# Layer norm of a macaron block: moments on ScalarE, reciprocal roots by GpSimd powers, and other places in the instruction order

## The chip, the cores and the metric

The kernel runs on one core of a Trainium2 chip. The core has five engines, each with its own instruction queue that is worked off in order: TensorE (PE in the profile, with its weight loads as PEld), VectorE (DVE), ScalarE (ACT), GpSimd (POOL) and SyncE (SP), which here issues the DMA transfers. An engine that waits for a semaphore holds everything behind it in its queue. The metric is the device time of one execution in microseconds, lower being better.

## The reference

The input is x, 2048 tokens of 512 float32 numbers. Three residual steps are computed:

```python
x = x + 0.5 * ffn(layernorm(x))
x = x + attention(layernorm(x))
x = x + 0.5 * ffn(layernorm(x))        # the same weights again

def layernorm(x): return (x - mean(x)) / sqrt(var(x) + 1e-5)

def ffn(x):       # Wg, Wu: 4096 x 512, Wd: 512 x 4096, each from 4-bit codes and a scale per 32 numbers
    gate, up = x @ Wg.T, x @ Wu.T
    return (gelu_tanh(gate) * up) @ Wd.T

def attention(x): # 16 heads of 32, causal softmax
    q, k, v = split(x @ Wqkv.T + bqkv)
    return softmax(q @ k.T / sqrt(32) + causal) @ v @ Wout.T + bout
```

Only the layer norms and the order of the work around them are touched by the change.

## The kernel before

**Tokens and phases.** The 2048 tokens are 16 tiles of 128 tokens (`xs`), and four blocks `tb` of 512 tokens (four tiles each). x stays in SBUF throughout. Three phases follow one another: `ffn(1, ...)`, `attention(...)` and `ffn(2, ...)`. Every phase starts from normalized and transposed tokens, `xT[tb]`.

**The norm of a block.** `norm_steps` returns a list of ten closures. `stats(0)` and `stats(2)` compute mean and variance of two tiles each on DVE (`bn_stats`, L88, and `bn_aggr`, L89); the second one then takes the square root of the four variances on ACT (L95), the reciprocal on DVE (L96) and, when the normalization is to run on ACT, minus mean times reciprocal on DVE (L98). `normalize(i)` writes the normalized tile `xn` (ACT at L105, or DVE at L107), into one of two buffers. `transpose(i)` transposes it by four matrix instructions into a PSUM bank (L115), which ACT copies into `xT` (L116). ACT holds one set of function tables at a time; the square root, GELU and exponential are in different sets, and each change of set shows as an `ACT_TABLE_LOAD`.

**An FFN phase.** The hidden size is cut into eight groups `g` with two halves each (`rows` and `second`), and the tokens into two pairs of blocks (`tp` 0: blocks 0 and 1, `tp` 1: blocks 2 and 3). `slot(g, rows, tp, ...)` computes gate and up of one half for one pair with Strassen's seven products instead of eight, so a slot has 14 products: seven for gate (`pg`, in the order 1, 2, 6, 7, 5, 4, 3) and seven for up (`pu`). A product is two calls, four matrix instructions of 128x512 in the profile, and takes one of seven PSUM banks (`ps_one`), which all phases share with the transposes. The right-hand factors are sums of token blocks, computed by `token_sums(tp)` on DVE (L256 to L259); products 1 and 2 need only the first block, product 6 needs the third sum. The products are combined by additions on DVE (L318 to L336), two copies on ACT (u2 after product 1, L315, with a single buffer; u4 after product 5, L327) and one addition on GpSimd (L330); GELU on ACT (L296) ends a gate cell and a multiplication with it on DVE (L300) ends an up cell.

In phase 1 the weights are first dequantized from their codes: ten steps on DVE per matrix half (L194 to L190), then four sums on GpSimd (L234 to L237). The weights are stored to DRAM and phase 2 reads them back, so that DVE and GpSimd have less to do there. Later halves are dequantized in the `background`: `slot` calls `pump(rate)` after every product, which takes so many steps from that list. `slot` also takes `groups`, lists of closures, and runs one group after each product. The down product is cut into 14 pieces (`down_pieces`, `po`, L375) that are either interleaved with a slot's products (`fill`) or, at the phase's end, run alone, with groups from `behind(normed)` between them.

**Where the norms stand.** At the start of phase 1 blocks 0 and 1 are normalized between the dequantization steps of the first half. The norms of blocks 2 and 3 are run by the groups `last_norms` of the second slot (`second`, pair 0), in the order that `paced` writes out: `[a0], [a1], [b0], [b1, an[0]], [an[1], at[0]], ...`, so moments, roots, normalizations and transposes all fall into that slot, and the token sums of pair 1 follow with its last product. Phase 2 does the same; its blocks 0 and 1 were normalized at the end of attention. The first two blocks of attention are normalized behind the last down pieces of phase 1 (`norms_behind`, also `paced`), and the first two blocks of phase 2 among the last steps of attention (L919 to L925), between the exponentials of the scores (L833) and the multiplications that form `attnT` (L779, on GpSimd, after reciprocals on DVE, L776). There the normalization is on DVE.

**Order.** The program is scheduled by hand: the order in which the Python code issues instructions is the order in each engine's queue. Waits are only added where data or buffers demand them.

## Time and profile before

| | us |
|---|---|
| median of three runs | 3295.69 |
| lowest and highest | 3292.89, 3295.72 |
| the profiled execution, its own time | 3295.73 |
| its span in the profile | 3294.0 |
| mean granted TensorE clock, share of full | 0.996 |

The page of the profile was taken on this one execution. Its first part gives the busy time of each engine; its second part cuts the span into 40 slices of 82 us. DVE is fullest in phase 1:

```profile
DVE  7877777877777556575655664554455455445545
ACT  4111111111111131464544455431111111111111
DMA  3111111111111100000000000101011101011101
```

Each digit is a busy share in tenths. Phase 1 takes slices 1 to 15, attention ends near the 26th, and phase 2 takes the rest. The most frequent instructions are these groups (line, engine, operation, output and inputs, count, then busy us, mean ns and the idle time ahead of them):

```profile
L375 PE MATMUL po<-wd,inter 128*128 128x256 f32 x2048 | 483.6, 380 | 0.0
L276 PE MATMUL pg<-xT_f,w 128*128 128x512 f32 x1024 | 480.9, 598 | 0.0
```

Matrix instructions are pipelined: four of one product are issued every 0.43 us, so a product takes 1.72 us though each one lasts some 0.6 us.

### The profile page before, as it was taken

How to read it: one execution, taken by the hardware profiler on the slowest of the kernel's cores; microseconds unless marked ns; L12 is line 12 of the kernel's file. 1: busy time of each engine (PE TensorE's matmuls, PEld its weight loads, DVE VectorE, ACT ScalarE, POOL GpSimd, SP SyncE). 2: the span in 40 equal slices, each digit the busy share in tenths (PEclk: the TensorE clock that was granted, in tenths of full speed). 3: DMA queues.
4: the chain of work that ended last, by engine and by line, in shares of the span. 5: the costliest groups of instructions: out<-in, count | busy, mean ns of one | idle time of the engine just before them, and what ended most of it. 6: DMA issues, size and time to landing. Idle time of an engine off the chain costs nothing.

```text
span 3294.0 us, 34151 instructions
## 1 busy us (share of the span) xinstructions
PE 3248.1 (99%) x12656; PEld 1724.3 (52%) x12656; DVE 2042.2 (62%) x3152; ACT 872.7 (26%) x1802; POOL 1127.8 (34%) x1319
## 2 busy tenths in 40 slices
PE   7999999999999999999999999999999999999999
PEld 3556565655656565333344333346555565656556
DVE  7877777877777556575655664554455455445545
ACT  4111111111111131464544455431111111111111
POOL 2546464554646331332212223113132222313222
PEclk9999999999999999999999999899999999999999
DMA  3111111111111100000000000101011101011101
GB/s 134 62 57 64 64 48 64 67 54 62 64 64 47 69 17 7 12 8 6 14 3 8 29 21 8 49 23 37 31 45 45 45 23 45 29 39 45 45 23 51
DMA packets 42055, 134.15 MB, mean 41 GB/s; under 512 B 5864, under 2 KB 26344, under 8 KB 35360
## 3 DMA queue, kind: packets, MB, share of 16 engines
q1 hardware_dynamic: 41888, 131.96, 11.0%
q8 instruction: 100, 1.64, 0.2%
q14 instruction: 67, 0.55, 0.1%
HBM read 81.91 MB, written 48.46 MB: 40 GB/s over the span
## 4 chain that ended last, share of the span: by engine, by line
PE 93%; DVE 3%; ACT 2%; issue 1%; POOL 1%; DMA 0%; SPq 0%; POOLq 0%; DVEq 0%; ACTq 0%
PE po L375 23%; PE pu L276 23%; PE pg L276 22%; PE av L740 8%; PE pm L675 6%; PE pqk L586 4%; PE ps L801 2%; PE pv L603 2%; PE pp L625 2%; PE ps L810 2%; ACT pt L833 1%; DVE st_f L88 0%; PE pt_f L115 0%; PE pt_a L115 0%; ACT both L749 0%
## 5 line engine op out<-in xcount | busy, mean ns | idle before, releaser
L375 PE MATMUL po<-wd,inter 128*128 128x256 f32 x2048 | 483.6, 380 | 0.0
L276 PE MATMUL pg<-xT_f,w 128*128 128x512 f32 x1024 | 480.9, 598 | 0.0
L276 PE MATMUL pu<-xT_f,w 128*128 128x512 f32 x1024 | 476.0, 592 | 0.0
L375 PEld LDWEIGHTS po<-wd,inter 128*128 128x128 f32 x2048 | 389.6, 190 | 155.4 <-issue 104.7
L690 DVE TENSOR_REDUCE parts<-pm 128x1 f32<-128x512 f32 (+3 forms) x640 | 370.4, 607 | 149.9 <-PE pm L675 134.6
L330 POOL TENSOR_TENSOR u<-u,u 128x512 f32<-128x512 f32 x128 | 163.7, 1279 | 865.5 <-ACT u L327 861.2
L389 POOL TENSOR_TENSOR x<-x,d 128x512 f32<-128x512 f32 x248 | 329.2, 1338 | 345.0 <-DVE d L383 171.7
L375 PE MATMUL po<-wd,s 128*128 128x256 f32 x1536 | 362.3, 379 | 0.0
L276 PE MATMUL pg<-xsum,w 128*128 128x512 f32 x768 | 357.4, 595 | 3.9 <-issue 2.0
L276 PE MATMUL pu<-xsum,w 128*128 128x512 f32 x768 | 355.7, 592 | 0.0
L375 PEld LDWEIGHTS po<-wd,s 128*128 128x128 f32 x1536 | 291.7, 190 | 116.2 <-issue 79.2
L675 PE MATMUL pm<-kT,qT 32*128 32x512 f32 (+3 forms) x1280 | 334.1, 574 | 0.1
L833 ACT ACTIVATE pt<-ps 128x512 f32<-128x512 f32 (+3 forms) x576 | 271.8, 533 | 130.3 <-PE ps L810 128.4
L740 PE MATMUL av<-pt,vaug 128*64 128x512 f32 (+3 forms) x1280 | 302.4, 557 | 3.1 <-ACT both L749 2.5
L276 PEld LDWEIGHTS pg<-xT_f,w 128*128 128x128 f32 x1024 | 195.8, 192 | 195.6 <-issue 181.8
L276 PEld LDWEIGHTS pu<-xT_f,w 128*128 128x128 f32 x1024 | 194.0, 190 | 189.9 <-issue 180.3
L810 PE MATMUL ps<-qT,kT 32*128 32x512 f32 (+3 forms) x1280 | 280.3, 539 | 0.0
L276 PEld LDWEIGHTS pg<-xsum,w 128*128 128x128 f32 x768 | 146.2, 191 | 151.5 <-issue 139.2
L276 PEld LDWEIGHTS pu<-xsum,w 128*128 128x128 f32 x768 | 145.5, 190 | 142.4 <-issue 135.4
L383 DVE SCALAR_TENSOR_TENSOR x<-po,x 128x512 f32<-128x512 f32 x192 | 131.4, 685 | 114.7 <-ACT d L397 85.6
L827 POOL TENSOR_SCALAR_AFFINE_SELECT pt<-pt 128x256 f32<-128x256 f32 x128 | 52.0, 406 | 401.2 <-ACT pt L826 400.4
L383 DVE SCALAR_TENSOR_TENSOR d<-po,d 128x512 f32<-128x512 f32 x192 | 131.6, 686 | 83.9 <-PE po L375 83.2
(128 smaller groups left out, 3601.6 us busy)
## 6 DMA issues: line engine op xcount, KB each, us to landing
kept<-wd SPq DMA_DIRECT2D x8, 1792.0 KB
wd<-kept SPq DMA_DIRECT2D x8, 1792.0 KB
x<-in_x SPq DMA_DIRECT2D x16, 256.0 KB
pk<-in_gate_codes SPq DMA_DIRECT2D x16, 256.0 KB
sc<-in_gate_scales SPq DMA_DIRECT2D x32, 128.0 KB
pk<-in_up_codes SPq DMA_DIRECT2D x16, 256.0 KB
sc<-in_up_scales SPq DMA_DIRECT2D x32, 128.0 KB
pk<-in_down_codes SPq DMA_DIRECT2D x16, 256.0 KB
```

The costliest lines, as they stand in the source:

```text
L276: nc.tensor.matmul(ps, lhsT=a[:, j, :], rhs=b[:, j, :], start=(j == 0), stop=(j == 1))
L330: nc.gpsimd.tensor_tensor(u4, u4, u2, ALU.add)
L375: nc.tensor.matmul(ps[:, j, :], lhsT=a[i][:, k, bass.ts(2 * q + j, P)], rhs=b[i][:, k, :], start=(k == 0), stop=(k == 1),)
L383: stt(dst, ps, 0.5, other, ALU.mult, ALU.add)
L389: adder.tensor_tensor(dst, dst, other, ALU.add)
L586: nc.tensor.matmul(ps, lhsT=w[:, j, k, :], rhs=xT[tb][:, k, :], start=(k == 0), stop=(k == 3))
L603: nc.tensor.matmul(ps[:, i, :], lhsT=xT[t // 4][:, k, (t % 4) * P : (t % 4 + 1) * P], rhs=wv_sb[:, k, bass.ts(half, 256)], start=(k == 0), ...
L675: nc.tensor.matmul(ps[a][:, :n], lhsT=q[r, bass.ts(4 * g + i, P)], rhs=k[r, kb * 512 : kb * 512 + n], start=True, stop=not on_pe,)
L690: nc.vector.tensor_reduce(parts[:, a, i, kb : kb + 1], ps[a][:, :n], AX.X, ALU.max)
L740: nc.tensor.matmul(av[64 * a : 64 * a + 64, off:], lhsT=vaug[:, c, p % 4, HD * a : HD * a + 2 * HD], rhs=pt[:, a, off:], start=(c == 0), s ...
L810: nc.tensor.matmul(ps[a][:, off:], lhsT=k[r, bass.ts(c, P)], rhs=q[r, g * 512 + off : (g + 1) * 512], start=False, stop=True,)
L833: nc.scalar.activation(pt[:, a, plain:], ps[a][:, plain:], AF.Exp, scale=scale)
```

## The change

`norm_steps` and `paced` become a class `Norm` with lists `moments`, `scales`, `normal` and `transposed`, and a function `staggered`, which interleaves two blocks' normalizations and transposes. New options are `moments_on_act` (sums and squared deviations as ACT instructions with an accumulated output, instead of `bn_stats` on DVE), `power` (the reciprocal root as an addition and a power -0.5 on GpSimd, instead of root on ACT and reciprocal on DVE), and `on_act` as the tiles that ACT normalizes.

```diff
+    expo = const.tile([P, 4], F32, tag="expo", name="expo")
+    nc.gpsimd.memset(expo, -0.5)
...
+        def __init__(self, phase, tb, t_out, temp, on_act=(0, 1, 2, 3), moments_on_act=False, power=False):
...
+            if moments_on_act:
+                def sums():
+                    for i in range(4):
+                        nc.scalar.activation(temp(f"sum_{nm}_{i}"), tiles[i], AF.Identity, accum_out=total[:, i : i + 1])
+                    nc.scalar.activation(total, total, AF.Identity, scale=-1.0 / D)
+                def squares():
+                    for i in range(4):
+                        nc.scalar.activation(
+                            temp(f"sq_{nm}_{i}"), tiles[i], AF.Square, bias=total[:, i : i + 1],
+                            accum_out=square[:, i : i + 1],
+                        )
+                self.moments = [sums, squares]
...
+            def scales():
+                if power:
+                    if moments_on_act:
+                        nc.gpsimd.tensor_scalar(rstd, square, 1.0 / D, EPS, ALU.mult, ALU.add)
+                    else:
+                        nc.gpsimd.tensor_scalar(rstd, mv[:, :, 1], EPS, None, ALU.add)
+                    nc.gpsimd.tensor_tensor(rstd, rstd, expo, ALU.pow)
+                    if moments_on_act:
+                        nc.gpsimd.tensor_tensor(nbias, total, rstd, ALU.mult)
+                    elif on_act:
+                        nc.gpsimd.tensor_scalar(nbias, mv[:, :, 0], -1.0, None, ALU.mult)
+                        nc.gpsimd.tensor_tensor(nbias, nbias, rstd, ALU.mult)
+                else:
+                    nc.scalar.activation(rstd, mv[:, :, 1], AF.Sqrt, bias=eps)
+                    nc.vector.reciprocal(rstd, rstd)
...
+    def staggered(a, b):
+        n, t = a.normal + b.normal, a.transposed + b.transposed
+        return [[n[0]]] + [[n[i + 1], t[i]] for i in range(7)] + [[t[7]]]
```

The other half of the diff changes where things are issued. In phase 1 the x tiles of block 1 are loaded ahead of the codes; block 1's moments come right behind block 0's norm, its normalizations (two on ACT, two on DVE) between the gate steps, and the token sums ahead of the up steps. Moments and scales of blocks 2 and 3 go into the first slot (`early`), their normalizations and transposes into the second from its first product on (`late`), with the token sums as groups of that slot. The down dequantization is put into the background before the second slot, at one step a product.

```diff
             if phase == 1:
+                load_x(1)
                 rows.load(0)
-                load_x(1)
                 rows.load(1)
...
-                run(norms[0][:2])
+                n0 = Norm("f1", 0, xT[0], normed)
+                n1 = Norm("f1", 1, xT[1], normed, on_act=(0, 1), power=True)
                 gate, up = rows.steps(0), rows.steps(1)
-                run(gate[:4])
-                run(norms[0][2:])
-                run(gate[4:])
-                run(norms[1][:2])
-                run(up[:4])
-                run(norms[1][2:])
-                run(up[4:10])
-                run(token_sums(0))
-                run(up[10:])
+                run(n0.steps() + n1.moments + [n1.scales] + gate[:5] + n1.tiles() + gate[5:])
+                run(token_sums(0) + up)
...
-            last_norms = paced(norms[2], norms[3])
-            sums = token_sums(1)
-            last_norms = [[]] + last_norms
-            last_norms[-1].append(sums[0])
-            last_norms.append(sums[1:])
+            n2, n3 = [
+                Norm(f"f{phase}", tb, xT[tb], normed, moments_on_act=True, power=True) for tb in (2, 3)
+            ]
+            early = [[]]
+            for n in (n2, n3):
+                early += [[n.moments[0]], [], [n.moments[1]], [], [n.scales]]
+            late = staggered(n2, n3) + [[s] for s in token_sums(1)]
...
-                    first = [slot(g, rows, 0, *fill, 2)]
+                    first = [slot(g, rows, 0, *fill, 2, early)]
                     pump(1 << 30)
-                    last = [slot(g, second, 0, [], [], 0, last_norms)]
...
+                if g == 0:
+                    last = [slot(g, second, 0, [], [], 1, late)]
-                first.append(slot(g, rows, 1, [], [], 1 if g > 0 else 2))
+                first.append(slot(g, rows, 1, [], [], 1))
```

At the two other seams, the end of phase 1 and the end of attention:

```diff
     def norms_behind(temp):
...
-        return paced(*[norm_steps("a", tb, xT_a[tb], temp, True) for tb in range(2)])
+        a, b = [Norm("a", tb, xT_a[tb], temp) for tb in range(2)]
+        tiles = staggered(a, b)
+        tiles[1].append(b.moments[1])
+        tiles[2].append(b.scales)
+        def scaled():
+            a.moments[1]()
+            a.scales()
+        return [[], [a.moments[0]], [scaled], [b.moments[0]]] + tiles
...
-                        steps = norm_steps(
-                            "f2", tb, xT_f[tb], lambda nm: an.tile([P, D], F32, tag="xn", name=nm)
+                        norm = Norm(
+                            "f2", tb, xT_f[tb], lambda nm: an.tile([P, D], F32, tag="xn", name=nm), (), power=True
                         )
-                        for i, step in enumerate(steps):
+                        for i, step in enumerate(norm.steps()):
```

Blocks 2 and 3 of attention use `Norm` with the old operations in the old order.

## The prediction

> **What bounds the kernel now.** I read the page first (busy shares and slices), then who PE waited for, then the timeline at each place where PE stops.
>
> ```profile
> PE 3248.1 (99%) x12656; PEld 1724.3 (52%) x12656; DVE 2042.2 (62%) x3152; ACT 872.7 (26%) x1802; POOL 1127.8 (34%) x1319
> PE   7999999999999999999999999999999999999999
> ```
>
> PE is the bound, and the change issues the same matrix instructions. It can win only PE's idle time, 3294.0 - 3248.1 = 46 us, and the slow matmuls after each stop, which count as busy.
>
> ```profile
> PE pt_f L115 <- ACT xn_f L105: 23.3, 6, 8.7
> PE ps L801 <- ACT pt L833: 4.1, 2, 2.6
> PE pt_a L115 <- ACT xn_a L105: 3.0, 2, 2.8
> PE pt_f L115 <- DVE xn_f L107: 2.0, 1, 2.0
> PE pg L276 <- DVE xsum L258: 1.9, 2, 1.0
> ```
>
> Nearly all of it is transposes of normalized tokens waiting for the norm (columns: total, times, longest). 8.7 of the 23.3 is the first load and cannot go. The timelines of the second slot of FFN 1, of FFN 1's end, of attention's end and of FFN 2's second slot show why:
>
> ```profile
> 61.77 1.28 ACT L95 ACT_TABLE_LOAD   x1
> 64.12 0.74 PE L115 MATMUL pt_f<-ident,xn_f 128*128 128x128 f32 x4 [4.29 <-ACT xn_f L105]
> 64.70 3.41 PE L276 MATMUL pg<-xT_f,w 128*128 128x512 f32 x4
> 88.10 3.70 PE L276 MATMUL pg<-xsum,w 128*128 128x512 f32 x8 [0.96 <-DVE xsum L258]
> ...
> 1178.90 0.30 ACT L95 ACTIVATE rstd_a<-mv_a,eps 128x4 f32<-128x4 f32 x1 [2.77 <-DVE mv_a L89]
> 1179.96 0.75 PE L115 MATMUL pt_a<-ident,xn_a 128*128 128x128 f32 x4 [2.79 <-ACT xn_a L105]
> ...
> 2073.95 0.30 ACT L95 ACTIVATE rstd_f<-mv_f,eps 128x4 f32<-128x4 f32 x1 [4.22 <-DVE mv_f L89]
> 2076.21 0.96 PE L801 MATMUL ps<-wo_bo,ones_b 3*128 3x512 bf16 x2 [2.63 <-ACT pt L833]
> 2092.01 0.87 PE L115 MATMUL pt_f<-ident,xn_f 128*128 128x128 f32 x4 [1.99 <-DVE xn_f L107]
> ...
> 2160.01 0.74 PE L115 MATMUL pt_f<-ident,xn_f 128*128 128x128 f32 x4 [4.29 <-ACT xn_f L105]
> ```
>
> Each time a square root sits in ACT's queue, waits for DVE's moments (4.22 us at 2073.95) and holds what stands behind it: normalizations, or the exponentials that free PSUM. After a stop PE is slow: the four matmuls at 64.70 take 3.41 us, elsewhere 1.72.
>
> At the start DVE is the second bound, which the windows by stage show (columns: us, then busy time of PE, PEld, DVE):
>
> ```profile
> 28.69:49.40 20.71, 20.71 (x50) 9.23 (x50) 20.43 (x32) 4.13 (x7) 7.30 (x7) 1.00 0.32 124
> ```
>
> DVE is as full as PE while the first products run (20.43 of 20.71).
>
> **What the Trainium skill says.** "ScalarE: Activation LUTs", What ACT_TABLE_LOAD costs: 1283 ns for every switch of set; the trace agrees (16 later loads, 1283 ns). The changed kernel issues 5 loads instead of 17. "TensorE: Matmul & The Clock Gate", Part 1: after an idle window of about 3.4 us the array runs at half clock until it has been busy as long; the doubled matmuls at 64.70 agree. "GPSIMD Engine Reference", 3.1: a two-input tensor_tensor costs about 2.6 cycles an element after a fixed dispatch; the trace has 205 ns for a 128x8 one. No page prices a power, and no run here shows one.
>
> **Part 1, start of FFN 1.** DVE begins at 3.50 as before and finishes block 0's moments and scales at 7.74. Block 1's moments now follow: 4 x 0.79 = 3.2, to 10.9 (its x tiles, now loaded ahead of the codes, are there: 8 tiles of 256 KB at about 300 GB/s land by 9; the gate codes are the ninth and land near 11). Five gate steps take 2.6, to 13.5. Then DVE normalizes tiles 2 and 3, but "xn" has two buffers, so it waits until PE has transposed tile 0, which ACT writes only after block 0's last copy (14.15): free at 15.6 and 16.3, done 16.8. Second half of gate 3.2: 20.0. PE starts there rather than at 23.08. Token sums 6.2, to 26.2; product 6 needs the third, at 24.6 (before 28.69: 4.1 earlier). But up's dequantization now stands after the sums: 5.9, to 32.1, before DVE's first eviction. DVE is 1.9 late (30.21 before). On SP's queue the next half's codes wait for the two code buffers: gate's is free near 18.7, up's near 31; with 3 us to land they are there before DVE's steps at 33 and 44. The store of the first weights now waits for up's sums on GpSimd, near 35 (29.16 before), and only the loads of the down codes stand behind it, wanted after 57.
>
> ACT then gets both blocks' moments in slot 0: per block four sums, a small one, four squares. I price a sum at 0.60 (GELU and copies of 128x512, back to back), a square with its pointer bias at 0.70 (normalizations 0.72): 2.4 + 0.25 + 2.8 = 5.5. Upper bound 0.9 each (an alone normalization 0.81 and something for handing over the sum); below 0.53 is excluded by the same rows. Queued behind them are PSUM copies that DVE needs. c11 33.8, its GELU 34.4, block 2's moments to 39.9, copy u4 40.5; c22 of product 5 waits for that (36.99 before), GpSimd's add 1.4 later, product 3's eviction 43.8, GELU 44.4, block 3's sums 47.1, copy of pu1 47.7, which DVE's next c11 waits for: 47.7 against 41.82. DVE needs 9.8 for the rest of slot 0 (11.2 before, 1.5 of it idle): 57.5; the next slot's c11 58.5, GELU 59.1, and behind it on ACT the second normalization 59.9. PE has by then done 3 of that slot's 14 products and one transpose; left are 11 x 1.72 + 7 x 0.46 = 22.1, to 82.0, and 1.8 for the slow clock (64.12 to 68.55 took 4.4 for 2.6 of work): 83.8 against 83.55. The token sums lie inside the slot now, so the 0.96 at 88.10 and its 0.1 go. **Part 1: 1 us gained**; bounds -4 (0.9 each) and +7.5 (nothing held up).
>
> **Part 2, end of FFN 1.** `n[0]` of block 0 is issued before block 1's square root, so ACT isn't held. Moments start one piece later (1172.7), scales 1177.3, first normalization 1178.3; its transpose follows piece 6, ending at 1168.37 + 6 x 1.72 = 1178.7: ready. Gone: 2.79, and the slow clock of 1179.96 to 1184.29 (4.33 for 0.46 + 1.72 + 0.46 = 2.64) and 0.1: **4.6 us** (3.5 to 4.8). Block 1's root comes after its moments were queued a piece before.
>
> **Part 3, attention's end.** Four table loads and two roots leave ACT; GpSimd gets an add and a power for each block. I take 1.0 us for the power: below 0.2 the 128x8 row excludes; upper 3. Exponentials run without the stop, so 2.63 and the slow iteration after it (L801 to L740, 6.1 for 3.1) go, but then GpSimd's attnT products and masks, late behind the power, hold ACT: I count a stop of 1.7 there and 0.5 at the next products. First block's second transpose 2083.0 instead of 2086.1 less jitter. The second block's chain is shown by DVE: moments 3.2 and root path 0.6 before, power path 1.2 now, so its transpose still waits 2.2 (2088.5 against 2092.01), but the exponentials of that iteration are done, so the 2.05 at L801 shrinks: the next transposes at 2093.8 against 2099.79. **6 us** (3 to 9).
>
> **Part 4, FFN 2.** DVE has slack here (16.05 of 28.0 in the first slot), so ACT's 11 us of moments only delay copies by 1 to 2.3 us, inside seven PSUM banks (7 x 1.72). Second slot: 2145.26 to 2179.55 is 34.3 for 14 x 1.72 + 8 x 0.46 = 27.8: 6.5, and 1.06 at 2184.10: **7.5 us** (6.5 to 8). The wait at 2122.89 (1.99, token sums behind the last attnT work on DVE) stays. Attention's own blocks 2 and 3 keep their order; the down dequantization starts a slot earlier at one step a product: 24 steps in 28 products, in time.
>
> Sum: 1 + 4.6 + 6 + 7.5 = 19.1; span 3294.0 - 19.1 = 3274.9, plus the profiled execution's 1.7 outside its span (3295.73) = 3276.6. That execution equals the median, 3295.69. **Forecast 3277.**
>
> **Rivals.** A, the forecast, 55%, own range 3271 to 3283. B, 20%: DVE's lag at the start isn't passed to PE (shorter sums, or products ahead far enough), so part 1 brings 7.5: 3270. For it: seven banks; against it: the GELU ahead of the second normalization. C, 19%: part 1 loses 4 and attention's end yields 3, because the in-order queues only hand the wait on: 3277 + 5 + 3 = 3285. For it: DVE's 20.43 of 20.71. D, 6%, slower than before: the power itself. Its place is GpSimd's queue, ahead of the transposes of both last blocks of attention and of block 1 at the start; each us above 1 costs about 3 us, so it decides from 1 + 19.1/3 = 7.4 us each; at 10 us 3277 + 27 = 3304. Against it: four elements a partition.
>
> **Numbers.** Below 0.2% (6.6 us) a measurement can't tell a change. Faster: A, B and 14 of C = 0.89; same: 5 of C and 2 of D = 0.07; slower 0.04. The range takes in A, most of B and most of C: 3265 to 3289.
>
> **What would show it.** Right: no PE wait over 1 us at the transposes of the two second slots in FFN 2 and at FFN 1's end; at the start product 6 near 25, DVE waiting for ACT's copies and a transpose near 60; five table loads; one wait of about 2 us left near attention's end. Wrong: sums on ACT far from 0.6, a power far from 1, or FFN 1's second slot ending before 79 or after 88.

## The result, and the profile after

The changed kernel takes 3283.53 us (median of six executions, 3282.66 to 3285.21). The kernel before, run beside it, lies between 3292.89 and 3297.02. The ratio is 0.9965, with a 95% interval of 0.9953 to 0.9978: 12 us are gained where 19 were forecast. The profiled execution took 3284.09 us, and its span is 3282.3.

On the page, PE's busy time and its slices:

```profile
PE 3239.4 (99%) x12656; PEld 1721.3 (52%) x12656; DVE 2027.8 (62%) x3110; ACT 875.7 (27%) x1849; POOL 1145.8 (35%) x1340
PE   6999999999999999999999999999999999999999
```

The count of matrix instructions is the same, and the first slice has lost a tenth while nothing else shows at this scale. Of the 11.7 us by which the span fell, PE's idle time gave only 3.0 (3294.0 - 3248.1 = 45.9 before, 42.9 after); the other 8.7 are busy time of the same instructions, which run slower for a while after some stops. So I cut both executions at the same PE instructions and compare the stretches. The first cut is what the experiments below call the marker: the start of product 6 in the third slot of FFN 1.

| stretch of PE's timeline | before | after | change | forecast |
|---|---|---|---|---|
| start to the marker | 88.10 | 94.78 | +6.68 | -1 (part 1) |
| to the first down piece that runs alone | 1080.27 | 1080.16 | -0.11 | |
| to the first query-key product | 32.64 | 27.94 | -4.70 | -4.6 (part 2) |
| to the last output projections | 905.68 | 900.09 | -5.59 | -6 (part 3) |
| to the first product of FFN 2 | 10.61 | 10.63 | +0.02 | |
| to product 6 of FFN 2's third slot | 66.80 | 58.96 | -7.84 | -7.5 (part 4) |
| to the end | 1109.86 | 1109.75 | -0.11 | |

The start fell short; in these two executions the other three parts came out within 0.5 us. Who PE waited for (total, times, longest) in the kernel after, with the rows left out that are alike before and after or under 1 us, except that of `pt_a`:

```profile
PE pt_f L150 <- ACT xn_f L142: 19.4, 7, 9.7
PE ps L835 <- ACT pt L867: 3.3, 2, 1.9
PE pt_f L150 <- DVE xn_f L144: 2.8, 1, 2.8
PE pg L315 <- POOL w L275: 1.9, 1, 1.9
PE pg L315 <- DVE w L229: 1.5, 1, 1.5
PE pu L315 <- DVE c L368: 1.3, 1, 1.3
PE pt_a L150 <- ACT xn_a L142: 0.2, 1, 0.2
```

The row of `pt_a`, 3.0 us before, is nearly gone. The first row has lost only 3.9 of 23.3, with 9.7 (8.7 before) now the first load. Three rows on products are new (behind GpSimd's and DVE's weights and a DVE addition); all lie in FFN 1's start. The timeline shows where each of the four places stands now (start, duration, engine and line, then in brackets the wait ahead of it; the places are FFN 1's second slot, FFN 1's end, attention's end and FFN 2's second slot):

```profile
58.15 1.13 PE L150 MATMUL pt_f<-ident,xn_f 128*128 128x128 f32 x4 [3.88 <-ACT xn_f L142]
59.07 3.62 PE L315 MATMUL pg<-xsum,w 128*128 128x512 f32 x4
65.42 1.13 PE L150 MATMUL pt_f<-ident,xn_f 128*128 128x128 f32 x4 [2.72 <-ACT xn_f L142]
66.34 3.62 PE L315 MATMUL pg<-xsum,w 128*128 128x512 f32 x4
...
1185.31 0.63 PE L150 MATMUL pt_a<-ident,xn_a 128*128 128x128 f32 x4
...
2081.75 0.21 PE L835 MATMUL ps<-wo_bo,ones_b 3*128 3x128 bf16 x1 [1.89 <-ACT pt L867]
2090.75 0.72 PE L150 MATMUL pt_f<-ident,xn_f 128*128 128x128 f32 x4 [2.82 <-DVE xn_f L144]
...
2153.08 0.74 PE L150 MATMUL pt_f<-ident,xn_f 128*128 128x128 f32 x4 [0.58 <-ACT xn_f L142]
```

FFN 1's end has no wait, FFN 2 one of 0.58, attention's end two of about the size before. Summed over both kinds, PE's waits at attention's end are the same as before: 3.3 + 2.8 against 4.1 + 2.0 us. FFN 1's second slot has two stops instead of one, and the four matrix instructions of a product at half speed after each. The window of the first slot (columns as in the prediction; DVE's busy time is the third) shows that DVE is no longer full there:

```profile
28.69:49.40 20.71, 19.02 (x45) 7.90 (x43) 17.05 (x27) 10.59 (x29) 8.33 (x11) 1.00 0.38 140
49.40:59.90 10.50, 5.90 (x15) 2.70 (x14) 9.21 (x15) 5.68 (x15) 4.48 (x6) 0.86 0.07 25
```

17.05 of 20.71, against 20.43 before: DVE now waits in this window, and PE stands still for 4.6 of the next 10.5 us. The following lines of the same timeline give the reason, in order:

```profile
17.15 0.55 DVE L144 TENSOR_SCALAR xn_f<-x,mv_f,rstd_f 128x512 f32<-128x512 f32 x1 [2.66 <-PE pt_f L150]
43.03 0.69 DVE L368 TENSOR_TENSOR c<-pg,u 128x512 f32<-128x512 f32 x1 [2.03 <-ACT u L366]
50.55 0.69 DVE L357 TENSOR_TENSOR c<-pu,u 128x512 f32<-128x512 f32 x1 [2.43 <-ACT u L354]
55.51 1.25 POOL L369 TENSOR_TENSOR u<-u,u 128x512 f32<-128x512 f32 x1
55.53 1.78 DVE L241 SCALAR_TENSOR_TENSOR val<-pk,val 128x512 uint32<-128x512 uint32 x1
56.80 0.59 ACT L354 COPY u<-pg 128x512 f32<-128x512 f32 x1 [2.98 <-POOL u L369]
57.28 0.82 ACT L142 ACTIVATE xn_f<-x,nbias_f,rstd_f 128x512 f32<-128x512 f32 x1
64.03 0.63 ACT L335 ACTIVATE c<-c 128x512 f32<-128x512 f32 x1 [5.93 <-DVE c L357]
64.56 0.80 ACT L142 ACTIVATE xn_f<-x,nbias_f,rstd_f 128x512 f32<-128x512 f32 x1
```

DVE stands 2.66 us at the start for an `xn` buffer. Later it stands 2.03 and 2.43 us for PSUM copies that are queued on ACT behind the moments. The u2 copy at 56.80 waits for GpSimd's addition, which frees the only u2 buffer and was itself queued behind block 3's power; the first normalization comes right behind that copy. The second normalization, at 64.56, is queued behind a GELU that waits 5.93 us for DVE.

### The profile page after: what moved, and what is told of

Read it like the earlier page. It is cut to its first block, busy times and chain, and to the rows that moved or that the text cites. A ratio compares the mean times of both kernels' runs of the same rounds, so it can differ in the third digit from the quotient of the medians.

```text
span 3282.3 us, 34191 instructions
## 1 busy us (share of the span) xinstructions
PE 3239.4 (99%) x12656; PEld 1721.3 (52%) x12656; DVE 2027.8 (62%) x3110; ACT 875.7 (27%) x1849; POOL 1145.8 (35%) x1340
## 4 chain that ended last, share of the span: by engine, by line
PE 94%; ACT 2%; DVE 2%; issue 1%; POOL 1%; DMA 0%; SPq 0%; POOLq 0%; DVEq 0%; ACTq 0%
PE po L414 23%; PE pu L315 23%; PE pg L315 23%; PE av L774 8%; PE pm L709 6%; PE pqk L620 4%; PE ps L835 2%; PE pv L637 2%; PE pp L659 2%; PE ps L844 1%; ACT pt L867 1%; PE pt_f L150 0%; ACT both L783 0%; PE pt_a L150 0%; POOL attnT L813 0%
```

## The experiments

Each kernel is the changed one with the edit shown. "Marker" is the first cut of the table above; it is read from one profiled execution of each kernel. The changed kernel and three others (both seams undone, and the two of FFN 2) have the same code up to the marker, and theirs are 94.78, 94.61, 94.17 and 93.57, so differences of about 1 us between markers tell nothing. The stretches from the marker up to attention were the same within 0.11 us in all runs with the same code there. Whole times also carry a variation in attention and FFN 2: 4.3 us between profiles whose attention differs in nothing, and 1.7 in FFN 2 (see the fourth and fifth experiments).

| kernel | median us (range, executions) | ratio to before, 95% | marker |
|---|---|---|---|
| changed kernel | 3283.53 (3282.66-3285.21, 6) | 0.9965 (0.9953-0.9978) | 94.78 |
| old start | 3281.20 (3280.42-3283.04, 5) | 0.9959 (0.9945-0.9973) | 89.25 |
| moments in pieces | 3282.44 (3281.23-3284.27, 5) | 0.9964 (0.9951-0.9977) | 90.06 |
| two normalizations ahead | 3277.44 (3276.73-3282.66, 4) | 0.9950 (0.9935-0.9965) | 89.43 |
| old start, pieces | 3277.41 (3276.32-3279.01, 4) | 0.9948 (0.9933-0.9963) | 86.67 |
| old start, pieces, two ahead | 3274.41 (3270.36-3276.45, 4) | 0.9933 (0.9917-0.9950) | 82.95 |
| mended start, pieces, two ahead | 3270.09 (3269.73-3274.32, 4) | 0.9927 (0.9913-0.9942) | 82.81 |
| ... and first two in the first slot | 3272.39 (3271.84-3274.88, 4) | 0.9932 (0.9917-0.9947) | 84.79 |
| ... and five ahead, in spare space | 3269.19 (3269.13-3271.86, 4) | 0.9925 (0.9908-0.9941) | 79.34 |
| FFN 1's norms as before, but a power | 3276.91 (3274.88-3277.41, 4) | 0.9945 (0.9930-0.9960) | 87.05 |
| both seams undone | 3292.41 (3290.62-3295.62, 12) | 0.9992 (0.9984-1.0001) | 94.61 |
| FFN 2: moments late, on DVE | 3287.43 (3285.15-3290.88, 10) | 0.9978 (0.9969-0.9987) | 94.17 |
| FFN 2: root early | 3283.34 (3282.83-3284.02, 6) | 0.9965 (0.9953-0.9978) | 93.57 |

### 1. FFN 1's start: its order, or the block of moments

The theory was that the new order of the start makes DVE late and that the undivided moments on ACT then hold the copies that DVE needs. One run puts the start's old order back, and with it block 1's old operations (square root, all four tiles on ACT):

```diff
-                load_x(1)
                 rows.load(0)
+                load_x(1)
...
-                run(n0.steps() + n1.moments + [n1.scales] + gate[:5] + n1.tiles() + gate[5:])
-                run(token_sums(0) + up)
+                run(n0[:2])
+                run(gate[:4])
+                run(n0[2:])
+                run(gate[4:])
+                run(n1[:2])
+                run(up[:4])
+                run(n1[2:])
+                run(up[4:10])
+                run(token_sums(0))
+                run(up[10:])
```

> The changed kernel with the start of FFN 1 in the order of the kernel before (loads, norms of blocks 0 and 1, gate, up and token sums), everything else as changed. Marker: start of product 6 of FFN 1's third slot, 88.10 us before and 94.78 changed. Theory (the reordered start makes VectorE late, and ScalarE's block of moments hands on and adds to the delay, about half each): VectorE's first eviction comes back from 35.5 to about 31.2, the marker to 86 to 89, the time to about 3277. Rival 1 (only the moments on ScalarE cost): marker within 2 us of 94.8, time 3282 to 3285. Rival 2 (only the start costs, the moments are hidden): marker near 80.6, time near 3269.5.

The second cuts the moments into pieces of two tiles, one piece behind each product, so that a copy should wait for two instructions instead of nine:

```diff
-                self.moments = [sums, squares]
+                self.moments = [
+                    lambda: sums((0, 1), False), lambda: sums((2, 3), True),
+                    lambda: squares((0, 1)), lambda: squares((2, 3)),
+                ]
...
-                early += [[n.moments[0]], [], [n.moments[1]], [], [n.scales]]
+                early += [[m] for m in n.moments] + [[n.scales]]
```

> The changed kernel with each block's moments on ScalarE cut into four groups of two tiles, one group after a product (sums of two tiles, sums of two, squares of two, squares of two, scales), so that at most about 1.5 us of them stand ahead of a PSUM copy; the start as changed. Theory (a whole block of 2.6 to 5.6 us ahead of the copies u4 and u2 holds VectorE): VectorE's waits for u4 (2.03) and u2 (2.43) and PE's for the second normalization (2.72) shrink, marker (94.78 changed) near 88, time 3276 to 3279. Rival (VectorE is simply late from the start, the waits only fill time in which it had nothing to give PE): marker within 2 us of 94.8, time 3282 to 3284.

The third does both:

> Old start and moments in groups of two tiles together. If both costs are real and separate, VectorE runs as in the kernel before without its 9.6 us of moments: second slot from about 49.4 without a wait of PE over 1 us, marker near 80.6 to 83, time 3269 to 3272, below both kernels. If only one of the two counts, the time is that of the better of the two single edits.

The markers are 89.25, 90.06 and 86.67. Against 94.78, the old start brings 5.5 us, the pieces 4.7, and both together 8.1, less than their sum of 10.2, which fits two causes on one chain, where either makes part of the other's gain. Together they beat the kernel before at the marker by only 1.4 us. The medians of the whole times gain less, 2.3, 1.1 and 6.1 us; in the profiles of the first two, attention took 2.5 and 1.4 us longer than in the changed kernel's, and FFN 2 of the second 1.7 longer. In the third kernel PE's timeline has this left:

```profile
52.73 0.63 PE L153 MATMUL pt_f<-ident,xn_f 128*128 128x128 f32 x4
53.19 1.88 PE L318 MATMUL pg<-xsum,w 128*128 128x512 f32 x4
58.10 0.75 PE L153 MATMUL pt_f<-ident,xn_f 128*128 128x128 f32 x4 [3.02 <-ACT xn_f L145]
58.69 3.39 PE L318 MATMUL pg<-xsum,w 128*128 128x512 f32 x4
```

The first transposes no longer wait. The second ones still do, for the normalization behind the GELU. I had expected 80.6 to 83 and missed this wait.

### 2. The normalization behind the GELU

The edit issues the second normalization ahead of that GELU, in the group with the first, in both FFNs:

```diff
-            late = staggered(n2, n3) + [[s] for s in token_sums(1)]
+            n, t = n2.normal + n3.normal, n2.transposed + n3.transposed
+            late = [[n[0], n[1]]] + [[t[i], n[i + 2]] for i in range(6)] + [[t[6]], [t[7]]]
+            late += [[s] for s in token_sums(1)]
```

> The changed kernel with one edit: in both FFNs the second normalization of the later tokens is issued together with the first (after the slot's first product), ahead of the GELU of c11 in ScalarE's queue; each further one stands behind the copy that frees its buffer. Theory: the 2.72 us wait of the second transposes goes, and the slow clock after it (3.62 for four products where 1.9 is usual) with it; the 3.88 us wait of the first transposes stays. Marker (product 6 of FFN 1's third slot) from 94.8 to 90 to 92, time 3279 to 3281. Rival: what is late there is DVE, not the order on ScalarE, and the wait comes back one transposes later or at the copies of the products: marker over 93.5, time 3282.5 to 3284.

> The old order of FFN 1's start, the ScalarE moments in pieces of two tiles, and two normalizations ahead. Theory: of the 86.7 us at the marker in the kernel with the first two edits, 3.0 (second transposes), 1.5 (slow clock after) and up to 0.6 (a later transposes) go: marker 81.5 to 83, time 3272 to 3274. Rival: the wait only moves: marker 85 or more, time over 3276.

Alone it moves the marker from 94.78 to 89.43: the wait of 2.72 at the second transposes is gone, a later one of 0.73 is left; the 3.88 at the first transposes stays, as expected, and the marker lies a little below the theory's 90 to 92. On top of the two edits before, it moves it from 86.67 to 82.95, in the theory's range.

A third kernel takes the new order of the start again, without its two mistakes. Block 1's normalizations are all on ACT, so that DVE waits for no buffer, and half of the up weights' dequantization fills the time until the transposed tokens are there:

```diff
-                n1 = Norm("f1", 1, xT[1], normed, on_act=(0, 1), power=True)
+                n1 = Norm("f1", 1, xT[1], normed, power=True)
...
-                run(token_sums(0) + up)
+                run(up[:5] + token_sums(0) + up[5:])
```

> As the one before, but with the new order of FFN 1's start, mended: block 1's four normalizations all on ScalarE (none on DVE waits for a buffer), and the first five steps of the up weights' dequantization ahead of the token sums, where DVE would wait for the transposed tokens. Theory: DVE loses its 2.7 and 0.3 us of waits and 1.1 us of work, c11 comes at 30 to 31.5 instead of 35.5, product 6 of the first slot at 25 to 27 instead of 26.8; marker = that + 53 = 78 to 81, time 3268 to 3271. Rival: the transposed tokens come later from ScalarE alone (its copies and normalizations are what PE waits for), product 6 at 28 or later, marker 82 or more, time no better than the old order's.

Product 6 starts at 26.19, inside the forecast, but the marker is at 82.81, no better than with the old order: 2.39 us of waiting at the first transposes came back. The whole time is still 4 us lower in the medians, 3270.09 against 3274.41, but the ranges overlap, and in the profiled executions attention alone differs by 4.3 us; the gain can't be given to the start.

### 3. What stands behind the last wait

In that kernel the first normalization, whose scales were ready at 44.2, was issued behind a u2 copy that waited 2.66 us for GpSimd's addition. The next edit issues the first two normalizations in the first slot, and block 3's power behind that addition:

```diff
+            early[-1:] = [[], [n3.scales, n2.normal[0], n2.normal[1]]]
...
-            late = [[n[0], n[1]]] + [[t[i], n[i + 2]] for i in range(6)] + [[t[6]], [t[7]]]
+            late = [[]] + [[t[i], n[i + 2]] for i in range(6)] + [[t[6]], [t[7]]]
```

> The mended kernel with one more edit: the first two normalizations are issued in the first slot (after its twelfth product), not behind the copy of the second slot's first product, and block 3's power comes with them, behind GpSimd's addition of that product instead of ahead of it. In the mended kernel the copy waits 2.66 us for that addition (one u2 buffer), and the normalization, whose scales were ready at 44.2, comes behind it at 52.0. Theory: the last wait at the transposes of FFN 1's second slot (2.39 us) and the slow clock after it (1.3) go: marker 82.8 to 79 to 80, time 3266 to 3268. Rival: the copies and DVE behind them are late anyway and the wait passes to a product: marker 81.5 or more, 3269 to 3271.

The theory failed, and the marker is in the rival's range. But the wait didn't pass to a product, as the rival had it: it passed to the third transposes and grew, and the marker rose to 84.79:

```profile
49.74 0.63 PE L153 MATMUL pt_f<-ident,xn_f 128*128 128x128 f32 x4
59.15 1.13 PE L153 MATMUL pt_f<-ident,xn_f 128*128 128x128 f32 x4 [4.88 <-ACT xn_f L145]
60.07 3.62 PE L318 MATMUL pg<-xT_f,w 128*128 128x512 f32 x4
```

With two buffers no third normalization can be issued ahead of the GELU, and DVE brings that GELU's input only at 57. The token sums of pair 1 have a tile that nothing uses until the transposes are done, so this edit normalizes block 2 into it and issues five normalizations ahead of the GELU:

```diff
+            sums1 = token_sums(1)
+
+            def spare(nm):
+                k = int(nm[-1])
+                return xsum[1][:, k // 2, k % 2, :] if nm.startswith("xn") else normed(nm)
...
+            late = [[n[2], n[3], n[4]], [t[0], n[5]], [t[1]], [t[2]], [t[3]], [t[4], n[6]], [t[5], n[7]], [t[6]], [t[7]]]
+            late += [[s] for s in sums1]
```

> The kernel of the run before the two of FFN 2 (mended start, moments in pieces of two tiles, first two normalizations in the first slot), and block 2's four normalized tiles go into the tile of pair 1's token sums, which is idle until then, so that two buffers no longer limit how far ahead they run; tiles 3, 4 and 5 are issued after the second slot's first product, ahead of the GELU of c11 (only the sixth behind it). Theory: what PE waited for (4.88 us at the third transposes, then 3.62 for four products instead of 1.9) was a normalization behind a GELU that waits for DVE at 57; with five normalizations ahead of it no transposes wait, marker 84.8 - 4.9 - 1.8 to 1.0 = 78 to 79.5, time 3265 to 3268. Rival: DVE, some 10 us behind PE at this place, is the bound itself, and with the transposes out of the way PE stops for PSUM banks that DVE hasn't read: a wait of 2 us or more at a product, marker 81.5 or more, 3269 or more.

The marker is at 79.34, inside the theory's range, and no wait over 0.4 us is left in the slot:

```profile
51.51 0.63 PE L153 MATMUL pt_f<-ident,xsum 128*128 128x128 f32 x4
53.70 0.63 PE L153 MATMUL pt_f<-ident,xsum 128*128 128x128 f32 x4
54.71 1.98 PE L318 MATMUL pg<-xT_f,w 128*128 128x512 f32 x4 [0.38 <-DVE u L378]
56.99 0.72 PE L153 MATMUL pt_f<-ident,xsum 128*128 128x128 f32 x4 [0.30 <-DVE c L360]
58.03 1.98 PE L318 MATMUL pg<-xsum,w 128*128 128x512 f32 x4 [0.32 <-ACT xT_f L154]
```

ACT's GELU still waits for DVE, until 56.88. PE's time goes down by 5.5 us all the same, although DVE's work is unchanged. So in this slot of this kernel DVE's lag reached PE only through ACT's queue, where normalizations stood behind a GELU; with them out of that queue place, the lag leaves PE waits of 0.3 to 0.4 us. At 3269.19 this kernel has the lowest median, 14 us below the changed one, though above the theory's 3265 to 3268 and in the rival's range. The marker alone gives 15.4; its attention took 2.0 us longer than in the changed kernel's profile and FFN 2 1.5 less. Against the mended kernel the marker is 3.5 us ahead and the median only 0.9, with attention 2.4 longer in the profile.

### 4. The seams

Both seams as before the change, the FFN parts as changed:

```diff
-                            "f2", tb, xT_f[tb], lambda nm: an.tile([P, D], F32, tag="xn", name=nm), (), power=True
+                            "f2", tb, xT_f[tb], lambda nm: an.tile([P, D], F32, tag="xn", name=nm), ()
...
-        tiles = staggered(a, b)
...
+        (a0, a1), (b0, b1) = a.steps()[:2], b.steps()[:2]
+        an, at, bn, bt = a.normal, a.transposed, b.normal, b.transposed
+        return [
+            [a0], [a1], [b0], [b1, an[0]], [an[1], at[0]], [an[2], at[1]], [an[3], at[2]],
+            [bn[0], at[3]], [bn[1], bt[0]], [bn[2], bt[1]], [bn[3], bt[2]], [bt[3]],
+        ]
```

> Both seams as before the change (attention's norm at the end of FFN 1 in its old order with the square root; FFN 2's first norms at the end of attention with the square root on ScalarE), both FFN parts as changed. Theory: the two seams are worth what the two traces show between them, 4.7 us up to the first product of queries and keys, 5.5 us up to the last output projection, and nothing else moves: about 3283.5 + 10.2 = 3293.7 us; the stretch from the first long down piece to the first query-key product goes from 27.9 back to 32.6 us, and the stretch of attention from 900 to 905.7. Rival: part of the gain at attention's end is the luck of that stretch (it was 900.1 to 902.6 in the runs with the same seam), so that undoing it costs only 2 to 3: 3290 to 3291.

The stretch to the first query-key product goes back from 27.94 to 32.67 us, to 0.03 of what it was. Attention's goes to 902.04, not to 905.7; the median, 3292.41, lies between theory and rival. So the attention part of the rival was right in this profile: undoing that seam cost 2 us. The windows from one and the same group of `av` instructions, ahead of the first stop, to the last projections show what differs. Each holds the same 152 matrix instructions; the columns are as in the prediction, PE's busy time second and the clock seventh. The kernel before, this run, the changed kernel, and two normalizations ahead (attention as in the changed kernel):

```profile
2070.27:2106.69 36.42, 31.48 (x157) 12.05 (x153) 13.80 (x30) 21.83 (x47) 5.05 (x11) 0.81 0.00 0
2076.43:2109.49 33.06, 27.50 (x157) 11.13 (x153) 13.81 (x30) 21.63 (x47) 5.05 (x11) 0.95 0.00 1
2072.01:2102.97 30.96, 26.00 (x156) 10.92 (x152) 13.78 (x28) 17.34 (x42) 7.57 (x15) 0.94 0.00 1
2067.18:2101.24 34.06, 29.11 (x157) 11.57 (x153) 13.78 (x28) 17.67 (x42) 7.55 (x15) 0.85 0.00 1
```

The first two have the same code here and differ by 3.4 us, at clocks of 0.81 and 0.95. The last two also have the same code and differ by 3.1, at 0.94 and 0.85. PE's idle time, the first number less the second, is 4.94 before and 4.96 after: the whole 5.5 us between those two windows is busy time. At about the same clock (second and third line) the new order wins 2.1 us. In the twelve profiles with the new order the stretch takes 30.8 to 31.1 us seven times, at 0.94 to 0.95, and up to 34.1 in the others, so two single executions of old and new order can differ by anything from -1 to 5.6, and the 5.6 of the first comparison is one draw. Whether the new order also makes the slow draws rarer is open. By the medians both seams together bring 3292.41 - 3283.53 = 8.9 us, of which the first is 4.7; that leaves an estimated 4.2 for attention's end.

### 5. What it was in FFN 2, and in FFN 1's root

The change does three things to FFN 2's norms of blocks 2 and 3: moments on ACT, powers on GpSimd, and moments and scales a slot earlier. One run keeps the power, but takes moments back to DVE and into the second slot:

```diff
-                Norm(f"f{phase}", tb, xT[tb], normed, moments_on_act=True, power=True) for tb in (2, 3)
+                Norm(f"f{phase}", tb, xT[tb], normed, moments_on_act=phase != 2, power=True) for tb in (2, 3)
...
+            if phase == 2:
...
+                early = []
+                late = [
+                    [], [a0], [a1], [b0], [b1, an[0]], [an[1], at[0]], [an[2], at[1]], [an[3], at[2]],
+                    [bn[0], at[3]], [bn[1], bt[0]], [bn[2], bt[1]], [bn[3], bt[2]], [bt[3], sums[0]], sums[1:],
+                ]
```

> The changed kernel with FFN 2 alone taken half back: moments on DVE in the second slot in the order of before, the power on GpSimd kept. It tells whether the gain of FFN 2 (from the first product to product 6 of the third slot 66.8 us before, 59.0 after; 1.7 of it clock at an unchanged wait) is that the root with its two table loads went, or that the moments went to the slot before. Theory: the place; the transposes still wait for DVE's moments and GpSimd's chain: 62 to 65 us for that stretch, time 3286.5 to 3289.5. Rival: the root's loads were the wait: 59 to 61 us, time 3283.5 to 3285.5.

The other takes moments and root back to DVE and ACT, but leaves them in the first slot:

```diff
+            on = phase == 1
             n2, n3 = [
-                Norm(f"f{phase}", tb, xT[tb], normed, moments_on_act=True, power=True) for tb in (2, 3)
+                Norm(f"f{phase}", tb, xT[tb], normed, moments_on_act=on, power=on) for tb in (2, 3)
             ]
```

> The changed kernel with FFN 2's norms of blocks 2 and 3 computed as before the change (moments on DVE, square root on ScalarE with its table loads, reciprocal on DVE), but in the places of the changed kernel: moments and scales in the first slot, normalizations from the second slot's first product on. Theory: the place is the whole gain, since ScalarE and DVE have room in FFN 2's first slot: that stretch 59 to 60 us as after, time within 1 us of the changed kernel's 3283.5, with four table loads more. Rival: the roots and loads hold GELU and the copies of products by 3 us twice and PE sees it: 61.5 us or more, 3286 or more.

The stretch from FFN 2's first product to product 6 of its third slot was 66.80 before and 58.96 after. It is 62.63 in the first run and 59.13 in the second, whose median of 3283.34 can't be told from the changed kernel's. So the earlier slot alone is enough for the whole gain of FFN 2, and there it doesn't matter which engine computes the moments and the root: the four extra table loads of the second run cost nothing that shows. The first run tells that the power does help in the late place: of the 66.80, 1.7 is a slow clock in the first slot, which it did not have, and 2.5 is left as the gain of the power; the earlier place brings 3.7 more. The chain on GpSimd and ACT shows why, with a power in the late place, PE still waits 1.92 us:

```profile
2147.38 0.23 POOL L123 TENSOR_SCALAR rstd_f<-mv_f 128x4 f32<-128x4 f32 x1 [9.59 <-DVE mv_f L113]
2147.69 1.04 POOL L124 TENSOR_TENSOR rstd_f<-rstd_f,expo 128x4 f32<-128x4 f32 x1
2150.09 0.63 ACT L335 ACTIVATE c<-c 128x512 f32<-128x512 f32 x1 [1.57 <-DVE c L368]
2150.62 0.80 ACT L142 ACTIVATE xn_f<-x,nbias_f,rstd_f 128x512 f32<-128x512 f32 x1
```

The scales are done at 2149.3, but the normalization again follows a GELU that waits for DVE.

For FFN 1 one run has the start as before, and the norms of blocks 2 and 3 too (moments on DVE, all in the second slot, the down dequantization behind it), with only the power in place of the root:

```diff
-                Norm(f"f{phase}", tb, xT[tb], normed, moments_on_act=True, power=True) for tb in (2, 3)
+                Norm(f"f{phase}", tb, xT[tb], normed, moments_on_act=phase != 1, power=True) for tb in (2, 3)
...
+            if phase == 1:
...
+                early = []
+                late = [
+                    [], [a0], [a1], [b0], [b1, an[0]], [an[1], at[0]], [an[2], at[1]], [an[3], at[2]],
...
-                    last = [slot(g, second, 0, [], [], 1, late)]
-                first.append(slot(g, rows, 1, [], [], 1))
+                    last = [slot(g, second, 0, [], [], phase - 1, late)]
+                first.append(slot(g, rows, 1, [], [], 1 if g > 0 else 2))
```

> In FFN 1 alone: old start, moments of blocks 2 and 3 on VectorE in the second slot in the old order (paced), no down dequantization beside them, but the reciprocal root by the GpSimd power; all else as changed. Tells the table loads and in-order roots from the place of the moments. Theory: the 4.29 us wait of the kernel before was the second block's root ahead of the first block's normalizations, so power alone takes most of it: marker near 82 to 84 (88.10 before), time 3271 to 3273. Rival (VectorE's own 9.6 us of moments set the wait): marker near 87 to 89, time about 3277.

The marker is 87.05, against 88.10 in the kernel before; the wait at the transposes is 2.57 us, where it was 4.29. So the rival was right: the power alone is worth 1.0 us there, no more than markers of equal code differ by, or 1.6 counted from the start of the second slot (49.37 before, 49.87 here). Its time, 3276.91, is 6.6 us below the changed kernel's. Whether DVE moments in FFN 1's first slot, where DVE is full, would do as well as in FFN 2 was not tried.

## Why the prediction was right and where it was wrong

**Parts 2 and 4** hold: 4.70 and 7.8 us against 4.6 and 7.5. Of FFN 2's 7.8, 1.7 came at an unchanged wait of 1.98 us: the eight matrix instructions after it took 5.37 us before and 3.67 after, so the second slot and the token sums behind it brought 6.1 of the 7.5, with a wait of 0.58 left there. The 1.7 was luck: in the kernel with moments in pieces the same wait was followed by the slow form again, and the stretch took 60.66. And the prediction gave ACT's moments and the powers a share that in FFN 2 the earlier place gives without them. The power was priced at 1.0 us; seven of them took 1.0 to 1.5.

**Part 3** came out at 5.6 against 6, but for more than half of it by luck. The prediction took the slow iteration after the stop of 2.63 us as a price that goes with the stop. In the run with both seams undone the old order has the same stop (2.62) and a clock of 1.00 in the 13.1 us after it, and at an equal clock the new order wins 2.1. What the prediction counted for the new order did come: a stop of about 1.7 (1.89), a second wait longer than before (2.2 forecast, 2.82 measured), and the 2.05 at L801 shrank (to 0.61). PE's idle time at attention's end stayed the same. The rest of the 5.6 is the draw of the clock.

**Part 1** is the step that failed: +1 forecast, -6.7 measured (-5.5 to -6.7 in the four profiles with that code, against the one before). Its mechanism is what the trace shows, the u4 and u2 copies behind the moments and a normalization behind the GELU of c11, and its two prices hold: a block of moments took 5.65 us against 5.5. The times in its chain slipped (ends, but for product 6, which is a start):

| step of part 1 | forecast | measured |
|---|---|---|
| gate weights done | 20.0 | 21.7 |
| product 6 of the first slot | 24.6 | 26.8 |
| up weights done | 32.1 | 34.2 |
| first c11 | 33.8 | 36.2 |
| u4 copy | 40.5 | 43.0 |
| copy of pu1 | 47.7 | 50.5 |
| c11 of the next slot | 58.5 | 64.0 |
| second normalization | 59.9 | 65.4 |
| second slot done | 83.8 | 91.4 |

Three terms of the sum, which make up most of the 7.6 us, were mis-sized.

- Some 2 us by the time that the up weights are done: DVE waited 1.19 us, until 6.28, for an x tile to land, where the prediction has block 0 done as before (it varied: 0.47 us in the last kernel of the third experiment, 1.42 in the mended one), and tile 2 got its `xn` buffer at 17.15 instead of 15.6.
- 2.7 more between the copy of pu1 and the next c11: "DVE needs 9.8 for the rest of slot 0 (11.2 before, 1.5 of it idle)". Before, DVE had no idle time between these two points (41.82 and 53.07), so 11.2 was all work. And the L241 at 55.53 took 1.78 us where 0.69 is usual, since it ran into GpSimd's addition. These are 1.4 and 1.1.
- 2.1 more to the slot's end: the slow clock after the second stop cost 2.6 (65.42 to 72.38), not 1.8, and the rest is a further wait of 0.58 at 75.31 and smaller losses around it and at 79.99.

The first stop of that slot, 3.88 us at 58.15, has no step in the prediction either: block 3's power on GpSimd holds the addition, which holds the one u2 buffer, which holds the u2 copy, and the first normalization is behind that on ACT. But it is no term of the sum: at the second normalization PE had done the three products and one transpose that the prediction has there, and in the kernel with two normalizations ahead this stop stays while the marker gains 5.3.

The experiments fit one chain: the old start, the pieces or two normalizations ahead each bring back about 5 us of the 6.7, all three 11.8. The last kernel shows the other side: rival B's premise, that DVE's lag needn't reach PE, is true in a kernel with the mended start and the pieces, once the normalizations don't stand behind the GELU. The forecast's own argument against B, "the GELU ahead of the second normalization", named the right place. With all these edits the marker of the kernel with five ahead is 8.8 us ahead of the kernel before's, where B gave part 1 a gain of 7.5.

The sum as a whole stayed inside the range because parts 2 and 4 were right and because the executions compared gave part 3 its number. Rival C's time, 3285, was nearer, and its reason, that the queues only hand the wait on, is close to what the runs show: part 1 lost more than its 4, and attention's end yielded 2.1 at an equal clock, or 4.2 by the medians, where C has 3. Rival D has no support: the power never took longer than 1.5 us.

## What to carry to other kernels

On an engine with an in-order queue, moving work earlier helps only if what stands behind it there can wait, and what stands ahead of it isn't itself waiting; cut such work into pieces of one or two instructions and put each behind something already released. When a second engine lags, ask through which queue the lag reaches the bound engine: in FFN 1's second slot it passed through ACT, and five normalizations issued ahead of one GELU left no wait over 0.4 us there without speeding up DVE. Before moving a computation to another engine to get rid of a wait, try the same computation in an earlier place: in FFN 2 that alone gave the whole gain. And before a difference between two profiles is given to a wait that went, take idle and busy time apart over the same instructions: at attention's end the idle time had not changed.

## What the runs showed of the hardware

- **Clock after a stop.** The same code after the same stop (1.88 and 1.89 us) gets different clocks at attention's end: in the changed kernel 1.00 in the 9.00 us up to the next stop, with two normalizations ahead 0.83 in 10.65 us, where the eight `qT,kT` instructions took 1.10 us instead of 0.71. The Trainium skill, "TensorE: Matmul & The Clock Gate", Part 1, says that the activity window of 3.4 us runs freely, so how many instructions run slow varies from run to run; these profiles agree with that. They also show slow instructions after stops shorter than that window, such as the 5.37 us after a stop of 1.99. The prediction counted such slow instructions as a fixed part of a stop's price. (Its 3.41 us against 1.72 sets a duration beside a spacing; in durations the four instructions took 3.41 against 1.88.)
- **DVE and GpSimd.** GpSimd's addition at 55.51 lasted 1.25 us, and the DVE instruction that started 0.02 us later took 1.78 instead of 0.69, ending 0.55 after the addition did. That is the exclusive lock that the Trainium skill, "SBUF — State Buffer", SBUF: two separate sides, describes for a DVE instruction with two SBUF inputs beside a GpSimd one. In the other direction, GpSimd's weight sums took 1.6 us beside DVE's token sums and 0.73 alone (old start and pieces).
- **Sums as a second output.** Every accumulating ACTIVATE is followed by an ACTIVATION_READ_ACCUMULATOR of 187 ns, which overlaps its neighbours: sums follow each other every 0.61 us and squares every 0.71, so the forecast's 0.60 and 0.70 were right without knowing of it.
- **Table loads.** The prediction's 1283 ns is the load alone. The page that it names, "ScalarE: Activation LUTs" of the Trainium skill, What ACT_TABLE_LOAD costs, adds about 1380 ns for draining the engine at every switch. No such time shows here: in the run with FFN 2's root early, the load starts at 2126.18, right behind a GELU, and takes 1.28 us, and the square root starts at 2127.47.
